# Two first stages by Strassen's scheme, sums in borrowed rooms, and another order of products in the last stage

## The chip, the cores and the metric

The kernel runs on one core of one Trainium2 chip. The metric is device time in microseconds, as the median of several runs. Five engines work side by side: TensorE (PE in the profile, its weight loads PEld), VectorE (DVE), ScalarE (ACT), GpSimd (POOL) and SyncE (SP). POOL issues DMAs on one queue, SP on a second, ACT on a third; the same 16 DMA engines serve all of them.

## The reference

Two layers of a graph network on 2048 nodes, 8 batches and 64 features, each with a residual and a layer norm. `adj` is 2048 x 2048. Cut to what is computed:

```python
# layer 0: K = 3 supports I, A, 2AA - I
As = [eye(N), A, 2.0 * (A @ A) - eye(N)]
w = einsum('nd,dkio->nkio', embedding, weight)      # weights of every node
x_g = einsum('knm,bmc->bnkc', stack(As), x)
out = einsum('bnki,nkio->bno', x_g, w) + einsum('nd,do->no', embedding, bias)
x = layernorm(x + out)
# layer 1: supports I, A, 2AA - I and softmax(relu(E @ E.T)), the same way, with its own weights
x = layernorm(x + out1)
```

The kernel never forms A @ A: it computes u = A x and then s = A u, and does so in each layer; the softmax support gives z.

## The kernel before, in words

**Layout.** x lies in SBUF as `x_all`, 16 slabs of 128 nodes x 512 (8 batches x 64 features) in float32, and u likewise as `u_all`. The nodes are cut into 8 blocks of 256, two slabs each. Both arrays are also scratch rooms at times when their content isn't needed: the sums of a right-hand side live in the other array or in `w_room` (16384 columns, the weights of one block's nodes).

**Stages.** There are 40 stages, 8 blocks in each of five phases (lines 724 to 730): A0 (stages 0 to 7, u = A x of layer 0), B0 (8 to 15, s = A u), A1 (16 to 23, u of layer 1), Z1 (24 to 31, the softmax support) and V1 (32 to 39, s of layer 1). A stage makes one block of a product of A with x or u. Besides, the weights of its nodes are made (`weights`, line 313), applied to the turned features (`apply`, line 334), and the result is normalized and stored (`post`, line 363).

**Plain and Strassen stages.** The set `plain` (line 220) names the stages that multiply straight: the first of each of A0, B0, A1, V1, and the second of A0. A plain A stage runs `straight` (line 445), 32 matmuls of 128 x 512; a plain B0 or V1 stage runs `turned` (line 580), 64 matmuls of 128 x 256 with slabs of u as the stationary side, in the order of the slabs. The others run `strassen` (line 465): both A's block and the right-hand side are cut in four quarters, and seven products p1 to p7 of eight k steps replace eight; in the `kk` phases (B0, V1) each k step is two matmuls of 128 x 128. A product takes one buffer of the PSUM pool `ps_acc` (two buffers); ScalarE copies p1 and p4 out, VectorE adds the others up (`add`). The order is p1, p4, p7, p2, p6, p5, p3. The right-hand side's sums T1 to T4 are made by `Sums.make` (line 695) on VectorE, over 128 x 2048 each; one of them (T2) overwrites a quarter of u in B0 and V1.

**Sums of A.** The combinations of A's quarters are made once, in phase A0, and kept in DRAM (`sd`): in a Strassen stage of A0 from the quarters in the stream, stored by POOL; in the second stage, which is plain, by `sums_of_a` (line 620), which has a tile with one buffer and stores by SP. B0, A1 and V1 read them back.

**Streams.** `adj` (lines 251 to 256) loads A's tiles of 512 KB through SP into four buffers, in an order written down beforehand; a tile is loaded when the buffer of the fourth before it is free. `wst` does the same for weights with three buffers, on SP too.[...]

**u's way.** In A0, u's place holds T1 to T4 of x. A block of u is therefore made in a tile of its own, stored to DRAM (`ud`) by POOL in `store_u` (line 460), and loaded into its place in the last A0 stage: `used` (line 563) loads two blocks each time a T has had its last use (T4: blocks 0 and 1; T3: 6; T2: 4 and 5; T1: 2 and 3), and block 7 follows in stage 8 (line 770). Z1's last pair of stages loads layer 1's u in the same way.

**The plan.** `put(n, i, f)` (line 743) writes a side job into stage n at place i of 64; the stage's own products pace it, and a job is issued when that share of the products has been. `spread` lays several jobs between two places. So the order of the instructions on every engine is fixed by these numbers. Around the change they are: the sums of u for B0 at places 51, 54, 60 of stage 8 and 0 of stage 9 (lines 765 to 767), those for V1 at 10, 20, 30 of stage 32 and 0 of stage 33 (775 to 777), `sums_of_a` at 10, 26, 42, 58 of stage 1 (787), the last stage's weights from 22 to 52 (811), one of its four applies at 60 (853), and the others and all of its normalization after the last product (869 to 875).

Of the kernel before, what the change touches and what calls it, by code (L numbers as in the profile page):

```python
# [48 lines left out]
def two_graph_layers(ctx: ExitStack, tc: tile.TileContext, x, x_t, adj_b, adj_q, layers, out):  # L49
# [170 lines left out]
    plain = {("A0", 1)} | {(phase, 0) for phase in ("A0", "B0", "A1", "V1")}  # L220
# [19 lines left out]
    def load_adj(t, key):  # L240
# [6 lines left out]
        else:  # L247
# [3 lines left out]
    lefts = [("quarter", (0, 0)), ("quarter", (1, 1)), ("sum", 2), ("quarter", (0, 1)), ("sum", 1), ("sum", 0), ("sum", 3)]  # L251
# [3 lines left out]
                 for key in ([("plain", j, i) for i in range(NJ // 4)] if (phase, j) in plain  # L255
                             else [(kind, j, i) for kind, i in (quarters if phase == "A0" else lefts)])])
# [5 lines left out]
    class Stage:  # L262
# [152 lines left out]
        def product(self):  # L415
# [9 lines left out]
            if self.n == 0:  # L425
                self.slabs = U[0:SB]
            else:
                made = one.tile([P, SB, BC], F32, tag="wraw", name="u")
                self.slabs = [made[:, s, :] for s in range(SB)]
# [30 lines left out]
        def store_u(self):  # L460
            if self.kk == 0:
                for s in range(SB):
                    (sp if self.li else pool).dma_start(out=ud[self.j][:, s, :], in_=self.slabs[s])

        def strassen(self, right):
# [5 lines left out]
            for i in range(4):  # L471
                rights[f"T{i + 1}"] = lambda k, i=i: sums[i](k)
            if self.wide:
                p1, p4, v = (four.tile([P, BC], F32, tag="f2k", name="temp") for _ in range(3))
                mine = {f"A{h + 1}{t + 1}": self.pair[h].quarters[t] for h in range(2) for t in range(2)}
            else:
                temps = one.tile([P, 4, half], F32, tag="wsplit", name="temps")
                p1, p4, v = (temps[:, i, :] for i in range(3))
                mine = {}
            made = {}  # L480
# [14 lines left out]
            def times(name, what, left):  # L495
                made[name] = acc = self.accumulator(name)[:, 0:2 * nodes]
                a = (mine[left] if inside else adj.next()).rearrange("p (k n) -> p k n", n=nodes)
                for k in range(k_slab):
                    if self.kk:
                        for q in range(2):  # L500
                            pe.matmul(acc[:, q * nodes:(q + 1) * nodes], rights[what](k)[:, q * P:(q + 1) * P],
                                      a[:, k, :], start=(k == 0 and q == 0), stop=(k == k_slab - 1 and q == 1))
                            yield nodes / NB
                    else:
                        pe.matmul(acc, a[:, k, :], rights[what](k), start=(k == 0), stop=(k == k_slab - 1))
                        yield 1
                if inside and name in ("p7", "p6", "p5", "p3"):
                    if streamed:
                        adj.held -= 1
                        adj.fill()  # L510
                    self.used(what)
# [15 lines left out]

            if inside:
                quarter("A11")
                quarter("A22")  # L530
            yield from times("p1", "B11", "A11")
            act.copy(p1, made["p1"])
            if inside:
                quarter("A21")
                sum_of_a(2, "A11", "A11", "A21", ALU.subtract)
                sum_of_a(0, "A21", "A21", "A22", ALU.add)
            yield from times("p4", "T4", "A22")
            self.used("T4")
            act.copy(p4, made["p4"])
            if inside:  # L540
                quarter("A12")
                sum_of_a(1, "A22", "A22", "A11", ALU.subtract)
            yield from times("p7", "T3", "A11")
            add(v, made["p7"], p1)
            add(p4, v, p4, ALU.subtract)
            yield from times("p2", "B21", "A12")
            add((0, 0), made["p2"], p1)
            if inside:
                sum_of_a(3, "A12", "A12", "A22", ALU.subtract)
            yield from times("p6", "T2", "A22")  # L550
            add(v, made["p6"], v)
            add(p1, made["p6"], p1)
            add((1, 0), made["p6"], p4)
            yield from times("p5", "T1", "A21")
            add(p1, made["p5"], p1)
            add((1, 1), made["p5"], v)
            self.repeat(1)
            yield from times("p3", "B22", "A12")
# [363 lines left out]
```

## Time and profile before

| what | value |
|---|---|
| time, median of 3 runs | 1472.86 us (1471.62 to 1473.08) |
| time of the profiled execution | 1472.41 us |
| its span, first to last instruction | 1470.6 us |
| PE busy | 1446.2 us, 98% |
| DVE busy | 952.9 us, 65% |
| ACT busy | 478.5 us, 33% |
| DMA | 282.85 MB, mean 192 GB/s |
| SP's queue | 171.99 MB |
| POOL's queue | 95.24 MB |

The profile comes from one execution; the sum of the prediction is made against that execution's own time. "Idle before, releaser" is the time an engine stood still ahead of an instruction, and what ended it. A plain line of the timeline is: start, duration, engine, line, operation, out<-in, shapes, how many merged. Nearly all instructions have line 43, since a helper records them, so the tiles' names tell them apart: `p` is a Strassen product, `pu` and `pz` a straight one, `po` an apply, `pw` weights, `pt` a transposition.

### The profile page before, as it was taken

The numbers are of one execution on the slowest core, as the hardware profiler recorded it, in microseconds if no ns is written. First come the engines' busy times: TensorE is split into PE (matmuls) and PEld (weight loads), VectorE is DVE, ScalarE is ACT, GpSimd is POOL, SyncE is SP. The second block draws the span as 40 slices with busy tenths as digits, with TensorE's granted clock in tenths as the row PEclk, the third lists the DMA queues.
The fourth block names the chain that finished last, engine by engine and source line by source line (L and its number), as shares of the span: only waits on it lengthen the run. The fifth ranks groups of instructions, "written<-read, shape, count | busy, mean of one in ns | idle before, by whom it ended". The sixth has DMA issues, their size and how long they took to land.

```text
span 1470.6 us, 31139 instructions
## 1 busy us (share of the span) xinstructions
PE 1446.2 (98%) x13310; PEld 1182.1 (80%) x13310; DVE 952.9 (65%) x1611; ACT 478.5 (33%) x594; POOL 205.4 (14%) x341
## 2 busy tenths in 40 slices
PE   9999999999999999999999999999999999999996
PEld 4577777778999998567877777788888888888885
DVE  3866666637666766865666667568783466666666
ACT  1444444432211213154444444432110233333332
POOL 5212221110111111111011111111000000000100
PEclk9999999999999999999999999999999999999998
DMA  9878888884666666477877878212213756665551
GB/s 359 279 260 273 286 284 266 275 316 158 206 191 205 205 205 194 159 176 196 194 197 190 180 212 209 52 51 79 69 58 107 218 180 198 192 188 192 192 188 57
DMA packets 86570, 282.85 MB, mean 192 GB/s; under 512 B 13984, under 2 KB 18080, under 8 KB 84832
## 3 DMA queue, kind: packets, MB, share of 16 engines
q1 hardware_dynamic: 53600, 171.99, 39.0%
q0 software_dynamic: 27360, 95.24, 21.1%
q10 hardware_dynamic: 5472, 13.63, 2.8%
q8 instruction: 105, 1.72, 0.5%
q14 instruction: 33, 0.27, 0.1%
HBM read 216.28 MB, written 60.83 MB: 188 GB/s over the span
## 4 chain that ended last, share of the span: by engine, by line
PE 92%; DVE 4%; issue 2%; DMA 1%; ACT 1%; ACTq 0%; DVEq 0%
PE p L43 56%; PE po L43 13%; PE pw L43 9%; PE pz L43 7%; PE pu L43 4%; PE pt L43 1%; DVE acc L43 1%; PE ps L43 1%; DVE u L43 1%; PE pr L43 1%; DMA x<-in_x 1%; DVE w L43 1%; ACT w L43 0%; ACT sq L43 0%; DVE t L43 0%
## 5 line engine op out<-in xcount | busy, mean ns | idle before, releaser
L43 ACT ACTIVATE w<-pw 128x1024 f32<-128x1024 f32 x330 | 320.1, 1022 | 434.9 <-PE pw L43 433.0
L43 DVE SCALAR_TENSOR_TENSOR acc<-po,mask,acc 128x256 f32<-128x256 f32 (+1 forms) x640 | 247.0, 426 | 74.4 <-PE po L43 57.3
L43 DVE COPY w<-pw 128x1024 f32<-128x1024 f32 x118 | 144.4, 1224 | 150.6 <-PE pw L43 150.3
L43 PE MATMUL p<-a,u 128*128 128x128 f32 x1792 | 219.0, 278 | 0.2 <-issue 0.2
L43 PEld LDWEIGHTS p<-a,u 128*128 128x128 f32 x1792 | 206.6, 192 | 8.1 <-issue 2.2
L43 PE MATMUL po<-w,t 128*32 128x256 f32 (+1 forms) x5120 | 206.2, 337 | 6.2 <-issue 6.2
L43 PE MATMUL p<-u,a 128*128 128x256 f32 x832 | 204.3, 388 | 0.0
L43 PEld LDWEIGHTS po<-w,t 128*32 128x32 f32 (+1 forms) x5120 | 127.2, 108 | 78.7 <-issue 16.2
L43 PEld LDWEIGHTS p<-u,a 128*128 128x128 f32 x832 | 151.6, 190 | 29.2 <-issue 5.4
L43 PE MATMUL p<-x,a 128*128 128x256 f32 x624 | 152.4, 384 | 0.0
L43 PEld LDWEIGHTS pw<-e,wst 64*128 64x128 f32 x1728 | 112.5, 184 | 45.5 <-issue 22.3
L43 PE MATMUL pw<-e,wst 64*128 64x256 f32 x1728 | 146.9, 297 | 2.0 <-ACT w L43 1.1
L43 PEld LDWEIGHTS p<-x,a 128*128 128x128 f32 x624 | 114.7, 190 | 19.3 <-issue 0.5
L43 PE MATMUL pu<-x,a 128*128 128x512 f32 x192 | 88.0, 606 | 0.4 <-DMA x<-in_x 0.3
L43 PE MATMUL p<-w,u 128*128 128x256 f32 x384 | 85.8, 379 | 0.0
L43 PE MATMUL p<-a,w 128*128 128x128 f32 x672 | 81.6, 277 | 0.0
L43 PE MATMUL p<-a,x 128*128 128x128 f32 x672 | 81.0, 277 | 0.0
L43 PEld LDWEIGHTS p<-w,u 128*128 128x128 f32 x384 | 72.1, 190 | 9.3
L43 PEld LDWEIGHTS p<-a,w 128*128 128x128 f32 x672 | 77.4, 192 | 2.6 <-issue 1.4
L43 PEld LDWEIGHTS p<-a,x 128*128 128x128 f32 x672 | 77.2, 192 | 1.9
L43 ACT ACTIVATE sq<-acc 128x1024 f32<-128x1024 f32 (+2 forms) x19 | 17.5, 922 | 159.0 <-DVE acc L43 146.4
L43 PEld LDWEIGHTS pu<-x,a 128*128 128x128 f32 x192 | 35.4, 192 | 41.7 <-issue 37.4
(123 smaller groups left out, 1435.5 us busy)
## 6 DMA issues: line engine op xcount, KB each, us to landing
wst<-wd SPq DMA_DIRECT2D x108, 512.0 KB, 6.4
a<-in_adj_q SPq DMA_DIRECT2D x87, 512.0 KB, 5.8
a<-sd SPq DMA_DIRECT2D x84, 512.0 KB, 4.2
sd<-a POOLq DMA_DIRECT2D x24, 512.0 KB, 6.2
a<-in_adj_b SPq DMA_DIRECT2D x16, 512.0 KB, 6.6
bx<-bx POOLq DMA_DIRECT2D x32, 256.0 KB, 5.4
acc<-bx POOLq DMA_DIRECT2D x16, 512.0 KB, 7.1
pd<-acc POOLq DMA_DIRECT2D x16, 512.0 KB, 4.7
```

What stands on the lines that cost most here:

```text
L43: return self._tc.keep_in_program_order(f(*args, **kwargs))
```

## The change

Five things are changed together.

1. Stage 8 (the first of B0) and stage 32 (the first of V1) run Strassen's scheme, with the products in the order 1, 2, 3, 4, 7, 6, 5: the first three use quarters of u itself. A fourth temporary keeps p3. In stage 8, product 1 takes the k steps in the order 0, 1, 4, 5, 6, 7, 2, 3.
2. They need sums of A's first block, so stage 0 makes and stores them as well.
3. The sums of u are made early in these stages: in stage 8 at places 6, 10, 20, 35 in a room inside x (`moved[0]`), for stages 8 and 9; in stage 9, SP copies them (3 DMAs of 1 MB) to `w_room`, where the later stages of B0 read them. In stage 32 they are made at 2, 6, 16, 26.
4. The last A0 stage writes u's last block straight into its place; its store and its load are gone.
5. The last stage takes its products in the order 1, 4, 7, 6, 5, 2, 3; its weights are made from place 12 to 42, applies 2 and 3 are issued at 50 and 55, the second half's normalization at 59, 61, 63, and applies 0 and 1 after the last product.

```diff
-    plain = {("A0", 1)} | {(phase, 0) for phase in ("A0", "B0", "A1", "V1")}
+    plain = {("A0", 0), ("A0", 1), ("A1", 0)}
+    factors = {1: (("quarter", (0, 0)), "A11", "B11"), 2: (("quarter", (0, 1)), "A12", "B21"), 3: (("sum", 3), "A12", "B22"),
+               4: (("quarter", (1, 1)), "A22", "T4"), 5: (("sum", 0), "A21", "T1"), 6: (("sum", 1), "A22", "T2"),
+               7: (("sum", 2), "A11", "T3")}
+    orders = {("B0", 0): (1, 2, 3, 4, 7, 6, 5), ("V1", 0): (1, 2, 3, 4, 7, 6, 5), ("V1", NBLK - 1): (1, 4, 7, 6, 5, 2, 3)}
+    usual = (1, 4, 7, 2, 6, 5, 3)
...
-            if self.n == 0:
-                self.slabs = U[0:SB]
+            if self.n == 0 or (self.phase, self.j) == ("A0", NBLK - 1):
+                self.slabs = U[SB * self.j:SB * self.j + SB]
...
-            if self.kk == 0:
+            if self.kk == 0 and self.slabs[0] is not U[-SB]:
                 for s in range(SB):
                     (sp if self.li else pool).dma_start(out=ud[self.j][:, s, :], in_=self.slabs[s])
...
+                ks = (0, 1, 4, 5, 6, 7, 2, 3) if (self.phase, p) == ("B0", 1) else range(k_slab)
+                for k in ks:
+                    start, stop = k == ks[0], k == ks[-1]
...
+            for p in order:
+                acc = yield from times(p)
...
+                elif p == 6:
+                    add(v, acc, v)
+                    u2 = w1 if order[-1] != 3 or order == usual else more
+                    add(u2, acc, w1)
+                    if order[-1] != 3:
+                        add(more, more, u2)
+                    add(c10, acc, w4)
+                elif p == 5:
+                    if order[-1] == 3:
+                        add(u2, acc, u2)
+                    else:
+                        add(c01, acc, more)
+                    add(c11, acc, v)
+                    self.repeat(1)
+                elif order[-1] == 3:
+                    add(c01, acc, u2)
+                else:
+                    act.copy(more, acc)
...
+    moved = flat_x[:, 2048:8192], w_room[:, 10240:16384]
+    for phase, slabs, room, n in (("B0", u_all, moved[1], 3), ("first", u_all, moved[0], 3), ("A1", x_all, flat_u, 4),
                                   ("V1", u_all, flat_x, 3)):
...
-        st.sums = sums.get(st.phase)
+        st.sums = sums.get("first" if st.n in (8, 9) else st.phase)
...
-    for i, place in ((0, 51), (3, 54), (2, 60)):
-        put(8, place, sums["B0"].make, i)
-    put(9, 0, sums["B0"].make, 1)
+    for i, place in ((0, 6), (3, 10), (2, 20), (1, 35)):
+        put(8, place, sums["first"].make, i)
+    for i in range(3):
+        part = slice(2048 * i, 2048 * i + 2048)
+        put(9, 30 + i, lambda part: sp.dma_start(out=moved[1][:, part], in_=moved[0][:, part]), part)
...
-    put(8, 2, load_u, (NBLK - 1,))
...
-    for i, place in ((0, 10), (2, 20), (3, 30)):
+    for i, place in ((0, 2), (3, 6), (2, 16), (1, 26)):
         put(32, place, sums["V1"].make, i)
-    put(33, 0, sums["V1"].make, 1)
...
-            for c in range(NJ // 4 if st.j == 1 else 0):
+            for c in range(NJ // 4 if st.plain else 0):
                 put(n, 16 * c + 10, st.sums_of_a, c)
...
-            spread(n, (22 if st.j else 4), (62 if st.j < 7 else 52), weights)
+            spread(n, (22 if 0 < st.j < 7 else 12 if st.j else 4), (62 if st.j < 7 else 42), weights)
...
-    put(len(stages) - 1, 60, last.apply, 2)
+    put(len(stages) - 1, 50, last.apply, 2)
+    put(len(stages) - 1, 55, last.apply, 3)
+    for part, place in enumerate((59, 61, 63)):
+        put(len(stages) - 1, place, last.post, part, 8, 16)
...
-    for c in (3, 0, 1):
-        last.apply(c)
-        if c == 0:
-            last.post(0, 8, 16)
-            last.post(1, 8, 16)
-    for part, g0, g1 in ((0, 0, 4), (2, 8, 16), (1, 0, 4), (0, 4, 8), (2, 0, 4), (1, 4, 8), (2, 4, 8)):
+    last.apply(0)
+    last.post(0, 0, 4)
+    last.apply(1)
+    for part, g0, g1 in ((1, 0, 4), (0, 4, 8), (2, 0, 4), (1, 4, 8), (2, 4, 8)):
         last.post(part, g0, g1)
```

## The prediction

> **What bounds the kernel now.** I read the page first (busy shares, the slices, the chain), then the groups with their shapes kept apart, then the DMA share in the stretches that the change touches, then the timelines of the two ends.
>
> From the page of the kernel before, busy time, slices and the chain by engine:
>
> ```profile
> span 1470.6 us, 31139 instructions
> PE 1446.2 (98%) x13310; PEld 1182.1 (80%) x13310; DVE 952.9 (65%) x1611; ACT 478.5 (33%) x594; POOL 205.4 (14%) x341
> PE   9999999999999999999999999999999999999996
> DMA  9878888884666666477877878212213756665551
> PE 92%; DVE 4%; issue 2%; DMA 1%; ACT 1%; ACTq 0%; DVEq 0%
> ```
>
> TensorE is the bound in every slice but the last, so an edit gains what it takes from TensorE, and loses whatever makes TensorE wait, at full price. The DMA row is at 8 or 9 for the first ten slices, all of the first phase: that is where new waits can come from.
>
> Groups by shape (engine, out<-in, count | busy us, mean ns of one):
>
> ```profile
> L43 PE MATMUL p<-a,u 128*128 128x128 f32 x1792 | 219.0, 278 | 0.2 <-issue 0.2
> L43 PE MATMUL pz<-a,u 128*128 128x256 f32 x256 | 59.2, 384 | 0.0
> ```
>
> Each matmul has two records. Means overlap, so I divide busy time by count: 0.231 us for a record of a plain first stage, 0.122 us for one of a Strassen stage.
>
> DMA share and GB/s (the two last columns) from 14 to 62 us, at the end of the last A0 stage (302 to 322), and in the second half of the second B0 stage (368 to 382):
>
> ```profile
> 14.00:62.00 48.00, 46.79 (x225) 22.95 (x227) 30.42 (x36) 19.10 (x21) 14.61 (x26) 1.00 1.03 370
> 302.00:322.00 20.00, 20.00 (x122) 16.46 (x122) 5.18 (x11) 8.29 (x9) 3.38 (x5) 1.00 0.93 326
> 368.00:382.00 14.00, 14.00 (x237) 13.68 (x236) 12.51 (x31) 2.65 (x3) 0.00 (x0) 1.00 0.36 123
> ```
>
> The DMA engines are full in the first two stretches and have room in the third.
>
> The instructions on the DRAM copy of u that start at 306.3 and 306.9: the two loads of u's blocks 2 and 3, issued when product 5 of the last A0 stage has ended:
>
> ```profile
> L43 SPq DMA_DIRECT2D u<-ud x2: 570/616/662, 306.3 to 306.9; - x2
> DMA to landing us min/median/max: 11.5/12.5/13.4
> ```
>
> They land at 317.8 and 320.3. The plain B0 stage starts at 309.2 and takes four slabs in some 8 us, so today nothing waits.
>
> VectorE, and then TensorE, in the second stage, around its first wait:
>
> ```profile
> 47.10 2.29 DVE L43 TENSOR_TENSOR u<-x,u 128x2048 f32<-128x2048 f32 x1
> 53.26 0.43 DVE L43 TENSOR_TENSOR sums<-a 128x256 f32<-128x256 f32 x1 [3.87 <-DMA sd<-sums]
> 54.73 2.28 DVE L43 TENSOR_TENSOR u<-x 128x2048 f32<-128x2048 f32 x1
> 57.02 1.39 DVE L43 COPY t<-pt 64x512 f32<-64x512 f32 x2
> ...
> 58.52 7.11 PE L43 MATMUL po<-w,t 128*32 128x256 f32 x128 [0.88 <-issue]
> ```
>
> The sums tile has one buffer: its next four sums wait until its store has landed (issued 44.9, landed 53.2). Behind them on VectorE stand T3 and the copies that TensorE's apply needs, and TensorE already waits 0.9 us there.
>
> [...]from 308 to 320 SP's and POOL's transfers advance together, about half each. [...]the trace has 3.2 when idle (u's blocks at 1117) and 11.5 to 13.4 when full. [...]what stands behind a waiting VectorE instruction waits too, as above.
>
> **The change, part by part.** The sum is made against the profiled execution: 1472.41 us, of which 1470.6 is the span; the median of the runs is 1472.86, 0.45 above.
>
> 1. Two plain stages become seven products. 128 records x 0.231 = 29.6 us become 128 x 0.122 + 96 x 0.121 (81.6 us of busy time over 672, the records on sums) = 27.3. Gain 2.3 each: -4.6.
>
> 2. u's blocks 2 and 3 at B0's start. Product 1 now wants them after six k: six times two matmuls of 0.226 (134 records took 15.16 us in the chain) = 2.7, and one group of weight matmuls, 1.0, so at 309.2 + 3.7 = 312.9. Block 2 lands at 317.8; then 0.45 for its k and 1.0 for the weights placed there bring TensorE to 319.2, and block 3 lands at 320.3, perhaps 0.7 earlier without the 512 KB store of u's last block (1.4 us at 385 GB/s, of which the load of acc takes most). Product 1 ends at 319.9 instead of 314.7: +5.2.[...] Bounds 3 and 6.5.
>    The chain behind it: T1 and T4 (2.3 + 4.6 us on VectorE) start at 319.6 and end by 326.7; product 4 wants them at 329.9. Hidden, 3 us to spare.
>
> 3. Sums of A in stage 0: four times four sums of 0.42 = 6.7 us of VectorE and four stores of 512 KB on SP, before the second stage's. DMA is full from 14 to 62, so every MB delays what follows by 2.7 us.
>    (a) Two stores come before x's last slabs: x 13 lands at 26.6, is wanted at 27.9; 26.6 + 2.7 = 29.3: TensorE waits 1.4.
>    (b) VectorE was idle until 25.7, which covers the first eight sums. The others, 3.4 us, and the weights that land 3 to 4 us later put the end of the weight splits from 43.3 to 48.3. The second stage's first sums then need the fourth store's landing (issued 42, 8 us as at 44.9): 50. Their own store (51.7) lands at 56 to 58.7, the next sums end at 58.7 to 60.4, T3 (2.3) and the copies (1.4) at 62.4 to 64.1. The apply that started at 58.52 starts then: +3.9 to +5.6, with (a) inside. I take +4.5. Below: if the stores landed as on an idle queue, only VectorE's own 3 us remain, less its idle 3.9 and with the store's latency as before: +1. Above: +6.5.
>
> 4. V1's first stage. u's blocks have landed by 1144.9, 3.5 us ahead of its start: no wait. But product 4's accumulator is that of product 2, whose addition stands on VectorE behind T1, T4 (6.9), T3 (2.3) and two weight copies (2.4): ready at 1162.5, wanted at 1162.0: 0.5. The next stage's first apply wants c11, now added last (four times 0.42 after product 5 plus 0.2, against 1.6 of matmuls): 0.3. Together +0.8; bounds 0 and 2.
>
> 5. The last stage. Product 5 ends one product earlier: 1445.84 - 3.6 = 1442.2. After it: product 2, apply 2, product 3, apply 3 end at +10.8. On VectorE the early normalization stands ahead of c01's addition: apply 2 (2.0), c00 (0.85), apply 3 (ends +9.65), the first post (1.6), then two round trips to ScalarE as at 1459 (0.74 and 0.36 idle) with 0.69, 0.2 and 0.69: +13.9. c01 ends at +14.75, so apply 0 starts 3.8 us after product 3. From there apply 0 1.8 on TensorE, 2.0 on VectorE, post 1.07, apply 1 2.0, and the same last 3.6 us of posts as before: +25.5, that is 1467.7 against 1467.5. +0.2. Were c01 ahead of the posts it would be -2.3; that and +1 are the bounds.
>
> 6. The moves: three of 1 MB on SP at about 368.1, behind one load. At 385 GB/s 8.2 us, at the 215 GB/s of the existing copies t<-t (4 KB packets of 0.305 us) 14.6. The next loads of A on the queue, issued at 373.4, are wanted at 384.2: they land at 381 or at 387. I take +0.3; bounds 0 and 3. POOL is idle there; x's first load into the moved rooms comes two stages later.
>
> 7. B0's second stage no longer starts with VectorE behind on T's (0.4 us in its weight matmuls): -0.3. u's last block stays in place; its store and load go, off the path. The 3 MB more of A in the two first stages ride three products ahead.
>
> Sum: -4.6 + 5.2 + 4.5 + 0.8 + 0.2 + 0.3 - 0.3 = +6.1: 1472.41 + 6.1 = **1478.5 us** (against the median the same sum reads 1479.0; I state the first).
>
> **Rivals.**
> - *The start is covered* (not slower). If the stores land in 4 us (the median of the four existing ones is 4.1), the apply waits about 1 us more: 1478.5 - 3.5 = 1475.0, and 1474.5 if x is not late either; it decides at about +1.2 of start cost, below which the sum is under 0.2%. For it: three of the four existing stores took 3.7 to 4.2 us. Against: the one in the full stretch took 8.3.
> - *SP's transfers come first* (faster). Were the engines to serve SP's queue ahead of POOL's, blocks 2 and 3 would land 3.1 MB / 385 GB/s = 8.2 us after 303, at 313: 5.2 gone, start 3.5 less: 1469.8. Against: the halves seen from 308 on. It decides when block 3 lands before about 314.
> - *The queue becomes the bound* (slower still). Moves at 215 GB/s, +2.7, and start at its upper end, +2: 1483.2; a second late load of A adds 2.
>
> **How the numbers follow.** Forecast 0.64 (its own range 1475.5 to 1482), start covered 0.16, SP first 0.10, queue bound 0.10. Low end 1472.0, which leaves SP first out; high end 1484.0, which leaves out half of the last: about 0.15 outside. 0.2% is 2.9 us, about what a measurement here can tell from no change. Faster: half of SP first and 0.01 of the start case, 0.06. Same: the other half, 0.12 of the start case, 0.02 of the forecast: 0.19. Slower 0.75.
>
> **What would show it.** TensorE waiting for a DMA of u some 3.7 us into the first B0 stage, 5 us long (step 2); the first apply of the second stage starting 4 to 6 us later, behind sums that wait for the sums' store (3); each changed first stage 2.3 us less of matmuls (1); in the tail, c01's addition after the early posts and some 4 us between product 3 and apply 0 (5); no wait for A at the third B0 stage (6). The prediction is wrong if the u wait is under 2 us, or if the second stage's apply moves by less than 2.

## The result and the profile after

The changed kernel takes 1482.47 us as the median of 4 runs (1482.19 to 1483.21), beside 1472.51 for the kernel before on the same chip (1471.62 to 1473.08). The ratio is 1.0069, with an interval of [1.0052, 1.0086]: slower by about 10 us. Measured a second time, on another chip, the ratio was 1.0088 [1.0071, 1.0105].

The profiled execution took 1482.61 us, its span 1480.8. From the page, the busy shares, and the slices with the granted clock and the DMA:

```profile
span 1480.8 us, 31584 instructions
PE 1448.7 (98%) x13502; PEld 1193.0 (81%) x13502; DVE 967.1 (65%) x1649; ACT 477.7 (32%) x596; POOL 204.2 (14%) x339
PE   9899999989999999999999999999999999999996
PEclk9999999999999999999999999999999999999998
DMA  9888897785876666478787888411313766666651
```

Two slices of TensorE fell from 9 to 8: the second (37 to 74 us), where the first stage ends, and the ninth (296 to 333), where stage 8 begins. TensorE's busy time did not fall by the 4.6 us of products saved; it rose by 2.5. The groups by shape (engine, out<-in, count | busy us, mean ns of one) show that the products themselves are not the reason:

```profile
L43 PE MATMUL p<-a,u 128*128 128x128 f32 x2048 | 252.0, 280 | 5.0 <-DMA u<-ud 5.0
L43 PE MATMUL p<-a,x 128*128 128x128 f32 x960 | 116.3, 278 | 0.0
```

A record of a Strassen product, of which each matmul has two, still costs 252.0 / 2048 = 0.123 us, against 0.122 before. The saving of products is there, then, and something else adds busy time. TensorE's longest waits (us in total, times, longest):

```profile
PE p L43 <- DMA u<-ud: 5.0, 1, 5.0
PE po L43 <- issue: 4.9, 7, 0.8
PE po L43 <- DVE t L43: 3.8, 1, 3.8
PE pw L43 <- DVE wsplit L43: 3.5, 1, 3.5
```

Three waits are new: for u's blocks, for the features `t` in the tail, and for the split weights of the first stage. Below are two stretches behind them, and one where the clock is whole, for the moves (start:end, length, busy time of PE, PEld, DVE, ACT and POOL, granted clock, DMA share, GB/s):

```profile
40.90:44.30 3.40, 3.40 (x7) 1.67 (x8) 3.30 (x4) 1.98 (x3) 2.88 (x6) 0.50 0.99 342
324.20:331.00 6.80, 5.73 (x30) 5.28 (x31) 3.36 (x2) 3.12 (x4) 0.00 (x0) 0.50 0.65 242
380.00:394.00 14.00, 14.00 (x236) 13.68 (x236) 12.47 (x30) 2.65 (x3) 0.00 (x0) 1.00 0.90 338
```

TensorE had half its clock for 3.4 and 6.8 us, at the end of the waits and just behind them, and once more for 3.4 us in the tail, and its instructions lasted longer there. Within these 13.7 us it was busy for 12.6; with the work taken to last twice as long at a clock of 0.50, an estimate of what half the clock adds is half of that, 6.3 us. That is most of the 7.1 us between the 4.6 that should have gone and the 2.5 that came. In the third stretch the moves of 3 MB fill the DMA engines (0.90 against 0.36 before) and TensorE is busy all the time.

Marks for the account are the starts of the applies (`po`) in the two traces:

| stretch, between apply starts | before | after | difference | forecast |
|---|---|---|---|---|
| start to stage 1's apply | 58.5 | 65.8 | +7.3 | +4.5 |
| stage 1's to stage 7's | 233.9 | 233.8 | -0.1 | 0 |
| stage 7's to stage 9's (292.4 to 362.3, 299.6 to 374.2) | 69.9 | 74.6 | +4.7 | +2.9, with the next row |
| stage 9's to the first of phase Z1 (to 946.3 and 957.4) | 584.0 | 583.2 | -0.8 | |
| from there to stage 33's (1183.8, 1192.7): V1's first stage | 237.5 | 235.3 | -2.2 | -1.5 |
| to stage 39's (1412.9, 1421.8) | 229.1 | 229.1 | 0 | 0 |
| from there to the end | 57.7 | 59.0 | +1.3 | +0.2 |
| sum | 1470.6 | 1480.8 | +10.2 | +6.1 |

**The start.** VectorE in the changed kernel: the end of the second of stage 0's four groups of sums, a split of the weights, and the third group (a line is start, duration, engine, line, operation, tiles, shapes, count, and the idle time before with what ended it):

```profile
26.84 0.42 DVE L43 TENSOR_TENSOR sums<-a,sums 128x256 f32<-128x256 f32 x1
...
28.70 1.22 DVE L43 TENSOR_TENSOR wsplit<-u,wsplit 32x1024 fp32r<-32x1024 f32 x1
36.62 0.43 DVE L43 TENSOR_TENSOR sums<-a 128x256 f32<-128x256 f32 x1 [6.71 <-DMA sd<-sums]
...
38.21 1.22 DVE L43 TENSOR_TENSOR wsplit<-u,wsplit 32x1024 fp32r<-32x1024 f32 x1
```

The two lines of `wsplit` are the two halves of one step. Between them stands the third group of sums, which waits until the store of the group before has landed (issued 27.3, landed 36.5: 9.2 us). The second group had waited for the first store in the same way: it starts at 25.71, the store landed at 25.63. TensorE at the same time, with the tail of the wait in the matmuls behind it:

```profile
35.58 0.38 PE L43 MATMUL pw<-e,wsplit 64*128 64x256 f32 x1
39.48 0.74 PE L43 MATMUL pw<-e,wsplit 64*128 64x256 f32 x7 [3.53 <-DVE wsplit L43]
40.89 0.80 PE L43 MATMUL pw<-e,wsplit 64*128 64x256 f32 x4 [0.67 <-DVE bx L43]
41.62 4.18 PE L43 MATMUL pu<-x,a 128*128 128x512 f32 x6
...
46.63 2.84 PE L43 MATMUL pu<-x,a 128*128 128x512 f32 x6
```

The six matmuls at 41.62 took 4.18 us, the same six at 46.63 took 2.84.

**u's blocks.** The landing times of the four loads from `ud` around this stage, and TensorE in the first stage of B0:

```profile
DMA to landing us min/median/max: 5.4/10.0/13.1
```

```profile
317.73 2.50 PE L43 MATMUL p<-a,u 128*128 128x128 f32 x20
325.27 0.80 PE L43 MATMUL p<-a,u 128*128 128x128 f32 x2 [5.05 <-DMA u<-ud]
326.00 1.65 PE L43 MATMUL pw<-e,wst 64*128 64x256 f32 x12
327.58 4.14 PE L43 MATMUL p<-a,u 128*128 128x128 f32 x20
331.65 0.98 PE L43 MATMUL pw<-e,wst 64*128 64x256 f32 x12
```

The forecast had the product end 5.2 us later; the wait is 5.05. Behind it 20 records took 4.14 us where 20 ahead of it took 2.50, and 12 weight records 1.65 where 12 later took 0.98.

**The tail.** VectorE ends the early normalization, then makes c01, and TensorE's apply 0 starts:

```profile
1465.08 0.69 DVE L43 TENSOR_TENSOR acc<-acc,rstd 128x512 f32<-128x512 f32 x1
1465.69 0.85 DVE L43 TENSOR_TENSOR t<-p,temps 64x256 f32<-64x256 f32 x2
```

```profile
1459.21 3.62 PE L43 MATMUL p<-a,u 128*128 128x128 f32 x30
1466.60 5.35 PE L43 MATMUL po<-w,t 128*32 128x256 f32 x64 [3.77 <-DVE t L43]
```

### The profile page after: what moved, and what is told of

Its sections match the earlier page's. It is cut to its first block, busy times and chain, and to the rows that moved or that the text cites. A ratio compares the mean times of both kernels' runs of the same rounds, so it can differ in the third digit from the quotient of the medians.

```text
span 1480.8 us, 31584 instructions
## 1 busy us (share of the span) xinstructions
PE 1448.7 (98%) x13502; PEld 1193.0 (81%) x13502; DVE 967.1 (65%) x1649; ACT 477.7 (32%) x596; POOL 204.2 (14%) x339
## 4 chain that ended last, share of the span: by engine, by line
PE 91%; DVE 4%; issue 2%; DMA 2%; ACT 1%; SPq 0%; DVEq 0%; ACTq 0%
PE p L43 59%; PE po L43 13%; PE pw L43 9%; PE pz L43 4%; PE pu L43 2%; PE pt L43 1%; DVE acc L43 1%; PE ps L43 1%; PE pr L43 1%; DVE u L43 1%; DMA u<-ud 1%; DMA sd<-sums 1%; DMA a<-in_adj_b 1%; DVE mean L43 0%; ACT w L43 0%
## 5 line engine op out<-in xcount | busy, mean ns | idle before, releaser
L43 PE MATMUL p<-a,u 128*128 128x128 f32 x2048 | 252.0, 280 | 5.0 <-DMA u<-ud 5.0
L43 PEld LDWEIGHTS p<-a,u 128*128 128x128 f32 x2048 | 237.8, 193 | 14.3 <-DMA u<-ud 5.2
L43 PE MATMUL p<-a,x 128*128 128x128 f32 x960 | 116.3, 278 | 0.0
L43 PEld LDWEIGHTS p<-a,x 128*128 128x128 f32 x960 | 110.5, 192 | 3.3 <-issue 0.6
L43 DVE TENSOR_TENSOR temps<-p,temps 128x256 f32<-128x256 f32 x114 | 45.5, 420 | 37.7 <-PE p L43 37.0
L43 PE MATMUL p<-a,w 128*128 128x128 f32 x576 | 70.0, 278 | 0.0
```

The source lines that it names most:

```text
L43: return self._tc.keep_in_program_order(f(*args, **kwargs))
```

## The experiments

Each kernel was measured beside the kernel before, on the same chip. Medians in us:

| run | what it is | median | before, beside it | ratio, interval |
|---|---|---|---|---|
| a_no_first_sums | changed, no sums in stage 0 | 1473.35 | 1471.70 | 1.0011 [1.0002, 1.0019] |
| i_own_rooms | changed, own rooms for these sums | 1477.39 | 1471.70 | 1.0041 [1.0026, 1.0056] |
| k_rooms_no_stores | the same without their stores | 1474.12 | 1471.45 | 1.0016 [1.0008, 1.0025] |
| b_first_sums_alone | before, plus sums in stage 0 | 1479.99 | 1471.95 | 1.0057 [1.0042, 1.0072] |
| d_earlier_loads | changed, u's blocks asked for earlier | 1477.11 | 1471.70 | 1.0042 [1.0026, 1.0057] |
| c_filled_wait | changed, filler matmuls (in too many places) | 1528.65 | 1471.70 | 1.0387 [1.0364, 1.0411] |
| c2_filled_wait | changed, filler in the u wait alone | 1482.07 | 1471.95 | 1.0071 [1.0055, 1.0086] |
| e_tail | changed, less ahead of c01 | 1480.60 | 1471.95 | 1.0061 [1.0046, 1.0076] |
| g_v1_alone | before, plus V1's first stage and the new tail | 1470.83 | 1471.95 | 0.9993 [0.9984, 1.0001] |
| after_again | changed, again | 1484.24 | 1471.66 | 1.0088 [1.0071, 1.0105] |
| j_three_mended | changed, with three mends | 1466.72 | 1471.66 | 0.9972 [0.9965, 0.9978] |
| h_v1_and_tail | g with the mended tail | 1466.49 | 1471.66 | 0.9960 [0.9947, 0.9972] |

**Is the start's cost that of stage 0's sums?** One run takes them out of the changed kernel, one puts them into the kernel before.

```diff
 # a_no_first_sums, against the changed kernel
-                "sum": lambda: sd[j][i]}[kind]()
+                "sum": lambda: sd[max(j, 1)][i]}[kind]()
...
-            for c in range(NJ // 4 if st.plain else 0):
+            for c in range(NJ // 4 if st.j == 1 else 0):
```

> The changed kernel, but stage 0 makes and stores no sums of A; the first stages of B0 and V1 read the second block's sums in their place, so the output is not the reference's and the work left out is the sixteen sums and four stores of stage 0. Theory (the start costs 7.3 us, as the first apply's start at 65.8 against 58.5 says): 1475.2 us, first apply again at 58.5, no drop of the granted clock before 300 us. Rival (most of the 7.3 us would be lost later anyway, because the DMA engines are full until 62 us): 1479 or more.

```diff
 # b_first_sums_alone, against the kernel before
-            for c in range(NJ // 4 if st.j == 1 else 0):
+            for c in range(NJ // 4 if st.j < 2 else 0):
```

> The kernel before, with the sums of A's first block made and stored in stage 0 as well, though nobody reads them; both first stages stay plain. Theory: the changed kernel's later start comes from these sums alone (their stores landing late in full queues, and the split of the weights queued on VectorE behind them): the first apply of stage 1 begins at 65 to 66 us (58.5 before), and the time is 1479 to 1480.5. Rival: the start is late because of the other edits, the new order of quarters and the readers of the sums; then this kernel stays within 1.5 us of the kernel before, at 1474 or less.

Without the sums the first apply starts at 58.7 us, 7.1 earlier, and the ratio falls from 1.0069 to 1.0011, some 8.5 us. The sums alone, read by nobody, put the kernel before at 1.0057, with the first apply at 68.1. Its waits show the same place:

```profile
38.79 1.09 PE L43 MATMUL pw<-e,wsplit 64*128 64x256 f32 x7 [3.50 <-DVE wsplit L43]
...
68.10 2.15 PE L43 MATMUL po<-w,t 128*32 128x256 f32 x36 [2.92 <-issue]
```

Both agree: the start is these sums, whoever reads them. They cost more than the two changed stages save.

**Is it the one buffer, the bytes, or VectorE's work?** In the next run the sums of stage 0 lie in four rooms (the old one, a part of u's place, two halves of a `t` tile), so none of them waits for a store; in the one after it the stores are left out too, and both first stages read the second block's sums.

```diff
 # i_own_rooms, against the changed kernel
-            r = one.tile([P, 4, 2, P], F32, tag="sq", name="sums")
+            if self.n == 0 and c:
+                if c == 2:
+                    rooms["t"] = two.tile([P, NB, B], F32, tag="t", name="sums")
+                flat = (u_all[:, 2:4, :].rearrange("p j x -> p (j x)") if c == 1 else
+                        rooms["t"].rearrange("p n b -> p (n b)")[:, 1024 * (c - 2):1024 * (c - 1)])
+                r = flat.rearrange("p (i k n) -> p i k n", i=4, k=2)
+            else:
+                r = one.tile([P, 4, 2, P], F32, tag="sq", name="sums")
 # k_rooms_no_stores, besides
-            sp.dma_start(out=sd[self.j]...
+            if self.n:
+                sp.dma_start(out=sd[self.j]...
```

> The changed kernel with a room of its own for each of the four sums of stage 0 (two in an idle tile of features, one in an unused part of u), so that no sum waits for the landing of the store before it; the same sums and stores. Theory (the single buffer is the cause): VectorE no longer stands still behind a store, the wait of the weights for their split is gone, and of the 7.3 us at the start at most 2.5 stay: 1477 us or a little over. Rival (the 2 MB of stores on full DMA engines are the cause, 2 MB at 380 GB/s being 5.5 us): 1481 us or more.

> The kernel of the run i_own_rooms without the four stores of stage 0's sums, 2 MB in all; the sums are still made on VectorE, and both first stages read the sums of A's second block instead. It splits what is left of the start once no instruction waits for a store any more. Theory: that rest is the 2 MB in queues that are full, which make the load of the running sum acc land late; without the stores the first apply of stage 1 has no wait in its middle, the first apply of stage 2 comes at 99 us as in the kernel before (103.1 with the stores), and the time falls by 4 us, to 1473 to 1474.5 (ratio to the kernel before 1.001 to 1.002). Rival: the rest is the 6.7 us of sums on VectorE; then stage 2's apply stays at 102 to 103 us and the time at 1477.

With rooms the wait for the split is gone, and the first apply starts at 58.8 us, as in the kernel before. But the time falls by some 4 us only. A smaller wait takes its place, in the middle of the first apply:

```profile
59.65 4.49 PE L43 MATMUL po<-w,t 128*32 128x256 f32 x79
66.37 2.98 PE L43 MATMUL po<-w,t 128*32 128x256 f32 x32 [2.22 <-DVE acc L43]
69.28 5.15 PE L43 MATMUL pu<-x,a 128*128 128x512 f32 x10
```

The addition into `acc` starts at 64.18, just after the load of `acc` has landed at 64.09, 11.0 us after its issue. POOL issued it at 53.08 (44.77 in the kernel before, where it took 9.6 us), since POOL had stood still ahead of it:

```profile
51.38 0.52 POOL L43 DMA_DIRECT2D t<-in_x_t  x1 [7.50 <-DMA sd<-sums]
```

This load goes into a `t` tile, and waited until the last store of stage 0's sums, which is made from its room in such a tile, had landed (issued 40.59, landed 50.80). The lent room was thus a lock of the same kind, on POOL instead of VectorE. The clock was at 0.5 from 67.1 to 70.5, and stage 2's apply started at 103.1 (98.8 before, 106.1 in the changed kernel). Without the stores POOL issued the load of `acc` at 46.64, it took 8.8 us and landed ahead of need, the apply ran through in one piece from 57.0, and stage 2's came at 97.3:

```profile
56.99 7.11 PE L43 MATMUL po<-w,t 128*32 128x256 f32 x128
```

So of some 8 us, by the medians, about half goes with the single buffer (4.1 us) and about half with the stores (3.7 us); the 6.7 us of sums on VectorE cost nothing that can be seen. By the start of stage 2's apply the two are 3.0 and 5.8 us, of which up to 1.8 us is the spread of the first apply's start between traces without the first wait (57.0 to 58.8). Whether the second half is the 2 MB in full queues or POOL's wait for the room is not shown, since the last run takes both away. Of what made the load of `acc` late, against the kernel before, 8.3 us are its later issue and 1.4 its longer way, which speaks for the room.

**Is the u wait a matter of when the loads are issued?** Stage 7's products in another order, so that T2's and T1's last uses, which free the loads, come before product 2.

```diff
 # d_earlier_loads, against the changed kernel
     orders = {("B0", 0): (1, 2, 3, 4, 7, 6, 5), ("V1", 0): (1, 2, 3, 4, 7, 6, 5), ("V1", NBLK - 1): (1, 4, 7, 6, 5, 2, 3),
+              ("A0", NBLK - 1): (1, 4, 7, 6, 5, 2, 3)}
...
-                if inside and p in (7, 6, 5, 3) and streamed:
+                if inside and p in ((7, 6, 5, 3) if order == usual else (7, 3)) and streamed:
...
+                    if streamed and order != usual:
+                        adj.held -= 2
+                        adj.fill()
```

> The changed kernel with the products of the last A0 stage in the order 1, 4, 7, 6, 5, 2, 3, so that the last use of T1 ends one product (3.6 us) earlier and the loads of u's blocks 2 and 3 are issued earlier; two tiles of A for the next stage are loaded a product later in exchange. Theory: the wait for u falls from 5.05 us to about 1, the clock doesn't drop, and the time falls by 7 us to 1475.5. Rival (the DMA engines are full, so that what is won for u is lost for A's tiles): TensorE waits for A's second tile, 1480 us or more.

The wait and the slow stretch behind it are gone; stage 8's apply comes at 340.2 instead of 346.3. A new wait of another kind stands ahead of it, for a sum of A that is now made right before its product:

```profile
309.33 3.62 PE L43 MATMUL p<-x,a 128*128 128x256 f32 x16
314.60 3.72 PE L43 MATMUL p<-x,a 128*128 128x256 f32 x16 [1.65 <-DVE a L43]
```

The old wait of 5.05 us and the 2.4 behind it (worked out below), less the new one of 1.65, make 5.8; the mark moved by 6.1. The time fell by about 4 us (1.0069 to 1.0042), short of the 7 that the theory named; the 1.65 was not in it.

**Is the slow stretch behind the u wait one of the clock?** Filler matmuls during the wait keep TensorE busy and give nothing else.

```diff
 # c2_filled_wait, against the changed kernel
                     start, stop = k == ks[0], k == ks[-1]
+                    if (self.phase, self.j, p, k) == ("B0", 0, 1, 2):
+                        idle_ps = big("pi")
+                        for _ in range(11):
+                            pe.matmul(idle_ps[:, 0, 0:256], ident, x_all[:, 0, 0:256], start=True, stop=True)
 # c_filled_wait had (self.phase, p, k) == ("B0", 1, 2) there
```

> The changed kernel with eleven matmuls of 128 x 256 without use put before the k step that waits for u's block 2, 4.75 us in a wait of 5.05. Theory (the clock that the profile shows at 0.5 from 324.2 to 331.1 us falls because TensorE stood still): the clock stays at 1.0 there and the time falls by 3.0 us to 1479.5. Rival (the clock falls for another reason, or the slow stretch is not what costs): no gain, 1482.5 us, or slower by whatever the filling overruns.

> The changed kernel with eleven needless products of 128x256 (float32, 0.43 us each, 4.8 us together) issued in stage 8 alone, between the second and the third k of p1, where the wait for u's block 2 lies. They only keep TensorE busy; the wait itself stays. Theory: the wait costs its length and, after it, 6.8 us at a granted clock of 0.5, which is another 3 us; with the filling the clock stays at 1.0 and the time falls by 2 to 3 us, to 1479.5 to 1480.5, first apply of stage 1 to that of stage 8 in 277.5 to 278.5 us (280.5 in the changed kernel). Rival: the matrix work after the wait is slow because the blocks have only just landed; then the p rows behind it stay as slow, and the time stays at 1482.5 or rises.

The first of the two had too wide a condition: it held in all eight B0 stages, so seven more carried 11 needless matmuls, with a wait of 5.9 us for x's loads in one place, and the time of 1528.65 says nothing on the question. (In stage 8 itself its trace is like the next one's: the clock is whole from 324 to 331, and from stage 1's apply to stage 8's it is 278.4 us.) The second has them in stage 8 alone. Two of its stretches, and TensorE in stage 8:

```profile
324.20:331.00 6.80, 6.31 (x52) 5.21 (x52) 2.67 (x2) 3.14 (x5) 0.00 (x0) 1.00 0.76 284
1463.50:1470.30 6.80, 5.35 (x52) 2.56 (x56) 2.91 (x7) 0.00 (x0) 0.00 (x0) 0.50 0.17 39
```

```profile
320.95 4.91 PE L43 MATMUL pi<-x,ident 128*128 128x256 f32 x22
326.15 0.49 PE L43 MATMUL p<-a,u 128*128 128x128 f32 x2 [0.28 <-DMA u<-ud]
...
328.17 2.27 PE L43 MATMUL p<-a,u 128*128 128x128 f32 x18 [0.21 <-DMA u<-ud]
330.37 0.97 PE L43 MATMUL pw<-e,wst 64*128 64x256 f32 x12
```

The blocks land as late as ever, and the same work behind them runs at full speed: from 326.15 to 330.37 less a wait of 0.21 it is 4.01 us, where the changed kernel took 325.27 to 331.65, 6.38. So 2.4 us of the cost was the clock. From stage 1's apply to stage 8's it is 278.5 us against 280.5. The rival, that blocks fresh from a DMA make the work slow, falls. The time of the whole kernel, though, did not fall (1.0071 against 1.0069): in the profiled execution the slow stretches at the start and in the tail were 6.8 us long each, where they had been 3.4, which gave back 0.7 and 1.1 us by the marks. That the saving doesn't show in the medians is within their intervals and stays open. The cost behind the wait also changes with the execution: the same 34 records took 5.65 to 6.74 us in the six traces of kernels with this wait and no filler, 1.6 to 2.7 more than 4.01, and not most behind the longest wait (after_again: wait 3.35, records 6.69).

**The tail.** Only the first of three parts of the early normalization stays ahead of c01.

```diff
 # e_tail, against the changed kernel
-    for part, place in enumerate((59, 61, 63)):
-        put(len(stages) - 1, place, last.post, part, 8, 16)
+    put(len(stages) - 1, 59, last.post, 0, 8, 16)
...
+    last.post(1, 8, 16)
+    last.post(2, 8, 16)
     last.apply(0)
```

> The changed kernel, of whose early normalization in the last stage only the first of three parts goes to VectorE ahead of the last product's additions; the other two follow them. Theory: TensorE's wait of 3.8 us ahead of the last second-slab apply is for those parts, so it falls below 1 us, the granted clock at 0.5 behind it goes with it, and the end comes 2.5 to 3.5 us earlier: 1479 to 1480. Rival: the end is set by VectorE's whole list of normalizations and the output stores, which only change places; then the time stays within 1 us of 1482.5.

```profile
1459.88 3.62 PE L43 MATMUL p<-a,u 128*128 128x128 f32 x30
1464.54 3.66 PE L43 MATMUL po<-w,t 128*32 128x256 f32 x64 [1.04 <-DVE t L43]
```

The wait falls from 3.77 to 1.04 and the apply behind it from 5.35 to 3.66, the half clock being gone there. From stage 39's apply to the end it is 55.6 us, against 59.0 in the changed kernel and 57.7 before: 3.4 less, of which 2.7 are the wait. The half clock is worth only the other 0.7, since the end hangs on VectorE, which begins to add while the apply still runs (in the changed kernel the apply goes from 1466.60 to 1471.95, and the first addition behind it starts at 1469.26). The run i_own_rooms shows the same: its wait here is 3.77 too, but no half clock followed, its apply took 3.66, and its last VectorE instruction ended 10.3 us after apply 0 had begun, against 11.0 in the changed kernel. The median fell less than expected (1.0061 against 1.0069), within the interval; the two runs with the same mend below show it more clearly.

**V1 alone, and what beats both.** V1's first stage by Strassen on the kernel before, with the sums of A's first block made in stage 8 from the plain tiles that it reads:

```diff
 # g_v1_alone, against the changed kernel
-    plain = {("A0", 0), ("A0", 1), ("A1", 0)}
+    plain = {("A0", 0), ("A0", 1), ("B0", 0), ("A1", 0)}
...
-            for c in range(NJ // 4 if st.plain else 0):
+            for c in range(NJ // 4 if st.j == 1 else 0):
...
+    for c, place in enumerate((6, 17, 19, 21)):
+        put(8, place, stages[8].sums_of_a, c)
 # and the sums of u for B0 at the places of the kernel before
 # h_v1_and_tail: with e_tail's tail
```

> The kernel before with Strassen's scheme in V1's first stage alone, and the changed kernel's last stage. B0's first stage is plain with the loads and sums of the kernel before, and the sums of A's first block are made in stage 8 out of the plain tiles that it reads, in four rooms of their own; stage 0 makes none, and nothing of u moves. Theory: V1's part is worth 2.2 us, the last stage costs 1.3 us, sums in stage 8 lie under TensorE's work, so the time is 1470.5 to 1472.5. Rival: the sums in stage 8 delay the stage's own additions or fill the queues as they did at the start, and it comes out at 1475 or more.

> The changed kernel once more, beside the two kernels that follow, so that they are compared on one chip. Expected: 1.0069 of the kernel before again, about 1482; the spells of granted clock at 0.5 behind the waits for the weights' split, for u's block 2 and for the early normalization are each 3.4 or 6.8 us long, and not the same ones in each execution, if their length is a matter of where a wait falls; a rival, that a wait fixes the length, expects 3.4, 6.8 and 3.4 us again.

> The changed kernel with three mends together: the sums of stage 0 in rooms of their own, stage 7's products in the order 1, 4, 7, 6, 5, 2, 3 so that u's blocks are asked for earlier, and two of the three parts of the early normalization behind the last product's additions. If the three causes are separate, their savings add: 4.5, 4.8 and 1.5 to 3.4 us off 1482, so 1469.5 to 1471.5, about the kernel before. If they share a cause (queues that are full until stage 8, or a later stage that waits for the same thing in any case), it stays at 1474 or more.

> V1's first stage alone by Strassen's scheme, as in the run named g_v1_alone, with the last stage's early normalization cut to one part ahead of the last additions. Theory: the gain of V1 (2.2 us) and a last stage without its wait of 3.8 us add up: 1467.5 to 1469.5, faster than the kernel before by 2.5 to 4 us. Rival: the last stage's end is set by the store of its output, and the wait only changes its place; then 1470.8 as without the cut.

V1's stretch is 235.2 us in both g and h, 2.3 less than before, with the sums of A costing nothing that can be seen in stage 8 (40.2 us from stage 7's apply to stage 8's in both, 40.4 before). g keeps the tail's wait and ends level with the kernel before. h has the short wait:

```profile
PE po L43 <- DVE t L43: 1.0, 1, 1.0
```

It takes 1466.49 us, ratio 0.9960 [0.9947, 0.9972], faster than both kernels. Expected was 1467.5 to 1469.5. From stage 39's apply to the end it is 55.4 us, 2.3 under the kernel before; with V1's 2.3 that is 4.6 of the 5.2 between the medians. The two gains add, as the theory had it.

The changed kernel with three mends comes to 1466.72 (0.9972), under the 1469.5 to 1471.5 expected: the savings add up, so the causes are separate. Taken singly the mends gave 0.0028, 0.0027 and 0.0008 of the ratio, together 0.0063; in one kernel they give 0.0097, from 1.0069. Part of the difference is the tail, whose mend was worth 3.4 us (0.0023) by its marks; the rest is within the intervals and isn't explained. Its trace still has waits of 2.4 us (`acc`) and 1.65 (`a`) that h's has not. That trace is of the longest of its 22 executions (1471.89), so it can't be summed against the median; but the medians say that B0's part, worth 2.3 us of products, ends at about nothing beside h.

The changed kernel again had slow stretches of 3.4, 6.8 and 3.4 us at the same three places. Its wait for u was 3.35 us rather than 5.05, and still 6.8 us of half clock went with it. That doesn't show that a wait fixes the length: other traces with the same waits have 6.8 at the start (d, b, c2) or nothing in the tail (i_own_rooms). The last section has what goes with it.

## Why the prediction was right, and where it was not

The direction and the range (1472 to 1484) held, and the three largest mechanisms that the forecast named are in the trace: the wait for u, the sums behind the landing of a store, and the wait in the tail. The size did not: 1478.5 for 1482.5. The likeliest case's own range, 1475.5 to 1482, was missed by 0.5, since the sum of +6.1 should have been +10.2. By its steps:

1. *Products, -2.3 each:* right. V1's stretch shows it (-2.2 in the changed kernel, -2.3 in g and h), and the records cost 0.123 us.
2. *u's blocks, +5.2:* right in place and in kind; the blocks landed 11.8 and 13.1 us after their issue, as they had before. That the wait is 5.05 in size is in part luck: in the six traces that have it, it is 3.35 to 5.05. What the step left out is the 2.4 us behind the wait.
3. *Sums in stage 0, +4.5:* the mechanism was there, the size wasn't, and it bit one step earlier. The working put the late stores into the second stage's first sums and the apply behind them, and let VectorE make the first eight sums in time in which it was idle anyway. But the one buffer also ties stage 0's groups to each other: the second began at 25.71, when the first store had landed, and the third at 36.62, when the second had. Since the third stands between the two halves of a weight split, the landing of the second store (9.2 us) held TensorE for 3.5 us at 36, and half clock followed, which is 1.3 us in the six matmuls after it. The splits ended at 53.96 and not at 48.3. The wait for x, 1.4 in (a), came as forecast and took 0.98. In place of +4.5 it measured +7.3 at the first apply; TensorE's idle time up to there rose by 4.7, its busy time by 2.5. That every MB delays what follows is not shown; the 2.7 us for one are an estimate at 385 GB/s, the rate that the trace of the kernel before has from 324 to 327 us. Of the four stores two took 10.7 and 9.2 us, two 3.2 and 5.8, and the run that could have weighed their bytes took a wait of POOL away with them. The working also misread the existing stores of the kernel before: two of the four, not one, lie in the full stretch, and they took 8.3 and 4.2 us.
4. *V1's waits, +0.8:* too much. Product 4's matmuls follow without an idle time; the stretch as a whole is -2.2, so at most 0.1 of the 0.8 is there.
5. *The tail, +0.2:* the wait was right to the tenth (3.8 forecast, 3.77 measured), and so was what it waits for. The stretch came to +1.3, and not mainly by the clock. Product 3 ended 41.05 us after stage 39's apply had started, where the working has 40.1: 0.9 of the 1.1 is there, ahead of the wait and at the full clock. The working took 3.6 us for a product; the last two took about 3.85 each. Behind the wait the half clock cost 0.7, but the items of the working there add up to 25.1 and not to its 25.5, and this slip hid more than half of it.
6. *The moves, +0.3:* right that little comes of them. They landed 5.8 to 10.8 us after their issue, the last of the 3 MB 12.0 us after the first issue, between the 8.2 us of 385 GB/s and the 14.6 of 215; the next load of A landed at 393.65, and TensorE was busy throughout.
7. *B0's second stage:* with step 1's half, 5.05 and 2.4, B0's beginning should be +5.1, and the marks have +4.7 up to stage 9's apply: nothing else of size hides there. The -0.8 after it was not traced; in traces whose code is the kernel before's in that stretch it takes 581.9 to 584.0 us (h, g, b and before), so it is within their spread.

By the table, the 4.1 us that the sum lacked are 2.8 at the start, 1.8 at B0's beginning and 1.1 in the tail, less 0.7 in V1 and 0.9 in the stretches that were forecast at nothing. The waits of TensorE themselves were priced about right (at the start its idle time rose by 4.7 for +4.5, then 5.05 for 5.2, 3.77 for 3.8), the first of them with another chain behind it. The step that failed is that every wait was priced at its length alone: behind these three the clock was at half for 13.7 us. It cost at least 1.3 us at the start, 2.4 behind the u wait and 0.7 in the tail. It wasn't the whole miss, since 0.9 us of the tail lies ahead of its wait, and it was in part offset by terms that came out better.

The rivals: "the start is covered" fell with runs a and b; "SP's transfers come first" fell with the u wait itself; "the queue becomes the bound" came nearest in time, 1483.2, and of its reasons only one is there: the start was at its upper end (+6.5 in the rival, +7.3 measured), but neither the moves nor a late load of A held TensorE. (In the second rival, 303 and 8.2 make 311.2, not 313; what decides, 314, is not touched by it.)

## What to carry to other kernels

Price a wait of TensorE at its length plus what the clock may take behind it: here 1.6 to 2.7 us behind waits of 3.4 to 5 us for u, 0.7 to the end of the kernel in the tail, where another engine sets the pace, and nothing where filler work covered the wait, or where an edge of the clock's windows (last section) cut its 3.77 us into 1.73 and 2.04. A tile with one buffer whose store goes into full queues was a lock here on what stood behind it in the engine's order (a store of 9.2 us, VectorE's wait of 6.71 for it, TensorE's of 3.53 behind that), so look for the nearest consumer, here the second half of a weight split, and not for the one that waited before. A room lent from another tile was such a lock too, on the engine that wanted that tile next (POOL, 7.50 us). And a gain that needs new data early can cost more in the full phase than it is worth: made in stage 0, the sums cost some 8.5 us for 4.6 of products saved; made in stage 8 from tiles that pass by anyway, the same sums cost nothing that could be seen (40.2 us between the applies, 40.4 before).

## What was not expected of the hardware

The granted clock. In the kernel before, the trace has a clock of 0.5 only from 1460.3 on, at the end. In the changed kernel it has it in three more places, each just behind a wait or from within it: 40.9 to 44.3 (behind 3.5 us), 324.2 to 331.0 (5.05), 1467.7 to 1471.1 (3.8). In all fourteen traces, the recorded changes of the clock lie whole multiples of 3.41 us apart, so each trace can be cut into such windows; in the changed kernel the first three stretches between changes are 34.13, 3.41 and 279.89 us, 10, 1 and 82 times 3.413. Four windows of i_own_rooms (the first number behind the length is TensorE's busy time, the third from the end the granted clock):

```profile
63.69:67.10 3.41, 1.19 (x27) 0.58 (x20) 2.78 (x6) 0.00 (x0) 0.00 (x0) 1.00 0.98 384
67.10:70.51 3.41, 3.41 (x26) 1.62 (x19) 3.23 (x8) 0.00 (x0) 0.00 (x0) 0.50 0.11 38
1456.33:1459.74 3.41, 1.68 (x15) 1.48 (x14) 2.48 (x5) 0.68 (x2) 0.00 (x0) 1.00 0.00 0
1459.74:1463.15 3.41, 1.38 (x28) 0.86 (x32) 1.65 (x4) 0.26 (x1) 0.00 (x0) 1.00 0.34 76
```

The wait of 2.22 us lay in one window, and the next had half the clock. The wait of 3.77 us in the tail was cut by a window's edge into 1.73 and 2.04, and the clock stayed whole; so was the 2.92 us of the sums alone, into 1.09 and 1.83, and d's 1.65 us was shorter than that.

Counted over the fourteen traces, the clock fell behind 40 windows; TensorE was idle for 2.07 us or more in 39 of them, and for 1.76 in the other one (c_filled_wait). In all the windows at full clock behind which it stayed whole, TensorE was idle for at most 2.04. In the changed kernel the four that it fell behind had 2.64 us (37.5 to 40.9), 3.41 (320.8 to 324.2), 2.31 (1464.3 to 1467.7) and 2.58 (1471.1 to 1474.5), and the others at most 1.55; in the kernel before the one had 3.38 (1456.9 to 1460.3), the others at most 1.41. So in these traces the idle time within one window goes with the fall, and not the length of a wait. A window at half clock in which TensorE worked throughout was never followed by a second one; all that were had idle time in them, 0.19 us or more. So it is with the 3.4 and the 6.8 us of the changed kernel: TensorE worked throughout from 40.9 to 44.3, and was idle for 1.04 us from 324.2 to 327.6. Where the edges lie differs from execution to execution: the first recorded change came at 4.1 to 6.9 us, 6.3 in the kernel before and 6.8 in the changed one. The ends of matmuls are modelled in the profile, so the border near 2.05 us is rough; and no run moved an edge on purpose, so this is read from the traces and not tested.
